# Layer 0 attention: exponentials grouped by tile of context, one addition for both tiles, another order on VectorE

## The chip, the cores and the metric

The kernel runs on one core of a Trainium2 chip. The metric is the time of one execution in device microseconds (us). A core has a matrix engine (TensorE, in the profile PE, its weight loads PEld), a vector engine (VectorE, DVE), a scalar engine for activations (ScalarE, ACT), a general engine (GpSimd, POOL) and a queue engine that here issues most transfers (SyncE, SP). Matmuls write into PSUM, 128 partitions with 8 banks of 512 fp32 each; VectorE and ScalarE read it, GpSimd doesn't. The other working memory is SBUF.

## What is computed

Two transformer layers on 16 batch elements of 256 tokens and 256 channels, all in fp32. Each layer has a self-attention, a cross-attention to a context of 256 tokens, and a feed-forward part, all with residuals. Layer 0, which the change is about, has 16 heads of 64 channels with rotary embedding:

```
def _attn(xq, ctx, wq, wkv, wo, bo):
    q = _heads(xq @ wq)
    k, v = jnp.split(ctx @ wkv, 2, axis=-1)
    k = _heads(k)
    v = _heads(v)
    q = _rope(q, sq, cq)
    k = _rope(k, sk, ck)
    sim = jnp.einsum('bhnd,bhmd->bhnm', q, k) * DH ** (-0.5)
    a = jax.nn.softmax(sim, axis=-1)
    o = jnp.einsum('bhnm,bhmd->bhnd', a, v)
    ...
    return o @ wo + bo

attn_in = _adaln(x, cond, ...)
x = _attn(attn_in, attn_in, sa_wq, sa_wkv, sa_wo, sa_bo) + x
cross_in = _adaln(x, cond, ...)
x = _attn(cross_in, _ln(context, ...), ca_wq, ca_wkv, ca_wo, ca_bo) + x
h = jax.nn.gelu(ffn_in @ ff_w1 + ff_b1, approximate=False)
x = h @ ff_w2 + ff_b2 + x
```

## The kernel before

The program is a sequence of six phases: self-attention, cross-attention and feed-forward of layer 0, then the same of layer 1. A phase has 16 jobs, one for each batch element. The main loop walks over steps; an attention job has two steps (s = 0, 1), a feed-forward job four. So layer 0 attention is 64 steps: 0 to 31 of self-attention, 32 to 63 of cross-attention. The order of the instructions on each engine is the order in which the program emits them, written out by hand; the semaphores between engines follow from the tiles (and PSUM banks) that instructions read and write. PSUM is one tile, `banks`, and the program names the bank of every product.

Scores are transposed: keys lie on partitions, in NT = 2 tiles of context of 128 keys, and the 256 queries along the free dimension. A unit u is four heads; a job has four units, a step handles two, u = 2s and 2s + 1.

- **`stage_s` (L585), the scores of a unit.** 64 matmuls (L598; here and below as the profile counts them, which shows each fp32 matmul twice) of 32 rows by 64 columns, for four heads into four banks: head h goes to bank `at + h`, the context's tile t into the columns t * 256 to t * 256 + 255. The loops run over t, then the half of the channels, then key group and head. The first unit of a step has banks 0 to 3, the second 4 to 7. Then two exponentials (L610), one for each pair p of heads: each reads two whole banks (1024 elements a partition) and writes a half tile `pr` of [P, 2, NT, N]. There are four such buffers. In layer 1 the first pair of every other unit is done head by head, which makes three exponentials.
- **`stage_t` (L614)** adds the two tiles of context for a pair of heads (L619, 512 elements) into half of `both` [P, 4, N]. **`stage_turn` (L621, L625)** transposes `both` in blocks of 32 into `squares`, and **`stage_reduce` (L629, L632)** sums each block's rows into `rows`, the softmax denominators. `both` and `squares` have one buffer each. All are on VectorE.
- **`layer0_sums` (L659)** multiplies `pr` by the values, 32 matmuls (L667) for a unit, into banks 4 and 5, and ScalarE copies the result out (L674). **`sum_up` (L634)** folds the denominators of the job before on PE, inverts them on VectorE (L641), and sends them by SP through memory to be spread (L644, L647). **`scale` (L651, L656)** multiplies by them on GpSimd.
- **`stage_rotary` (L539)** makes queries and keys for the unit of the following step, by products (L82, in `product`) into bank `2 * e + half`: the first unit e = 0 in banks 0 and 1, the second in banks 2 and 3. The keys come first, into columns 256 to 511 (`pq[:, 1, :]`), then the queries. For self-attention that is 64 matmuls for a unit; for cross-attention a part of the keys' product is made ahead by `start_keys` (L527, matmuls L534), 8 matmuls for a unit, right behind the scores. VectorE multiplies by cosine and sine (L555, two for each call, into `m0` and `m1`, two buffers each), and after the second half GpSimd adds and subtracts (L563, two for a unit) into `qk`.
- **`scores(i)` (L1057)** runs `stage_s` for both units of a step, and then `start_keys` for the step behind it where that is cross-attention.
- **`finish_folded` (L946)** in odd steps multiplies the job before by the output weights with seven block products (L82, `folded_w` and `wo` in the profile) in banks 4 and 5, and VectorE adds them to x (L958 to L965). The factors are made by GpSimd (`fold_inner`, L944).
- **`pair_hidden` (L802)**, in the feed-forward phases, has three sums in the buffers of `pr`: `copy` and `six` in one half tile, `seven` in another.

The part of the main loop for layer 0 attention sets the order in a step: VectorE gets two additions, the transpose, two L555, an addition, two L555, an addition, four L555, the reduction, the transpose, the reduction, and then `finish_folded`'s additions (odd steps) or the next job's moments (even steps).

Of the kernel before, what the change touches and what calls it, by code (L numbers as in the profile page):

```python
# [10 lines left out]
F32 = mybir.dt.float32  # L11
I32 = mybir.dt.int32
AF = mybir.ActivationFunctionType
ALU = mybir.AluOpType
AX = mybir.AxisListType

P = 128
N = 256
# [5 lines left out]
NT = N // P  # L24
# [19 lines left out]
def fast(ctx: ExitStack, tc: tile.TileContext, a: dict, out: bass.AP, flag):  # L44
# [4 lines left out]
    nc = tc.nc  # L49
# [6 lines left out]
    work = ctx.enter_context(tc.tile_pool(name="work", bufs=2))  # L56
# [5 lines left out]
    banks = psum.tile([P, 8, 512], F32, name="banks")  # L62
# [521 lines left out]

    def stage_s(job, u, at):  # L585

        key = job["key"]
        pair = job["qk"].pop(u)
        for t in range(NT):
            for half in range(2 if job["layer"] == 0 else 1):  # L590
                for g, h in [(g, h) for g in range(2) for h in range(4)]:
                    r = slice(32 * h, 32 * h + 32)
                    keys = slice(t * P + 64 * g, t * P + 64 * g + 64)
                    if job["layer"] == 0:
                        lhs, rhs = pair[half][r, 1, keys], pair[half][r, 0, :]
                    else:
                        lhs, rhs = pair[1][r, keys], pair[0][r, :]
                    nc.tensor.matmul(  # L598
                        banks[64 * g : 64 * g + 64, at + h, t * N : (t + 1) * N], lhs, rhs,
                        start=(half == 0), stop=(half == 1 or job["layer"] == 1),  # L600
                    )
        prs = []
        for p in range(2):
            pr = work.tile([P, 2, NT, N], F32, tag="pr", name=f"pr_{key}_{u}_{p}", bufs=4)
            sc = banks[:, at + 2 * p : at + 2 * p + 2, :].rearrange("p h (t n) -> p h t n", n=N)

            parts = 2 if job["layer"] == 1 and u % 2 == 0 and p == 0 else 1
            for i in range(parts):
                one = slice(i, i + 1) if parts == 2 else slice(0, 2)
                nc.scalar.activation(pr[:, one], sc[:, one], AF.Exp, scale=0.125 if job["layer"] == 0 else 0.25)  # L610
            prs.append(pr)
        job["pr"][u] = prs

    def stage_t(job, u, p):  # L614

        pr = job["pr"][u][p]
        if p == 0:
            job["both"] = work.tile([P, 4, N], F32, tag="both", name=f"both_{job['key']}_{u}", bufs=1)
        nc.vector.tensor_tensor(job["both"][:, 2 * p : 2 * p + 2, :], pr[:, :, 0, :], pr[:, :, 1, :], ALU.add)  # L619

    def stage_turn(job, u):  # L621

# [6 lines left out]
    def stage_reduce(job, u):  # L629
        if u == 0:  # L630
            job["rows"] = work.tile([P, 4, 32], F32, tag="inv", name=f"rows_{job['key']}")
        nc.vector.tensor_reduce(job["rows"][:, u, :], job.pop("squares"), AX.X, ALU.add)  # L632
# [25 lines left out]

    def layer0_sums(job, u, at):  # L659

        key, v, prs = job["key"], job["v"], job["pr"].pop(u)
        o = bank(at, 2, N)
        for half in range(2):
            for t in range(NT):
                for h in range(4):
                    col = (4 * u + h) * 64 + 32 * half
                    nc.tensor.matmul(  # L667
                        o[32 * h : 32 * h + 32, half, :], v[:, t, col : col + 32], prs[h // 2][:, h % 2, t, :],
                        start=(t == 0), stop=(t == NT - 1),
                    )  # L670
        if u % 2 == 0:
            job["halves"].append(work.tile([P, 4, N], F32, tag="part", name=f"raw_{key}_{u}", bufs=4))
        raw = job["halves"][-1][:, 2 * (u % 2) : 2 * (u % 2) + 2, :]
        nc.scalar.copy(raw, o)  # L674
        job["raw"].append(raw)

    def layer1_sums(job, c, e, at):

        key, v, prs = job["key"], job["v"], job["pr"].pop(2 * c + e)
        o = bank(at, N)  # L680
        for t in range(NT):
            for h in range(4):
                nc.tensor.matmul(  # L683
                    o[32 * h : 32 * h + 32], v[:, t, 4 * c + h, 32 * e : 32 * e + 32],
                    prs[h // 2][:, h % 2, t, :], start=(t == 0), stop=(t == NT - 1),
                )

        if c == 0 and e == 0:  # L690
            job["parts"].append(work.tile([P, 4, N], F32, tag="part", name=f"oT_{key}", bufs=4)[:, 0:2, :])
            job["sums"] = work.tile([P, N], F32, tag="inv", name=f"sums_{key}")
        raw, sums = job["parts"][0][:, c, :], job["sums"]
        if e == 0:
            nc.scalar.activation(raw, o, AF.Copy, scale=mask[:, 0:1])
        else:
            nc.vector.scalar_tensor_tensor(raw, o, mask[:, 1:2], raw, ALU.mult, ALU.add)
        eighth = mask[:, 4 - 2 * e + c : 5 - 2 * e + c]
        if c == 0 and e == 0:
            nc.scalar.activation(sums, o, AF.Copy, scale=eighth)  # L700
        else:
            nc.vector.scalar_tensor_tensor(sums, o, eighth, sums, ALU.mult, ALU.add)
# [99 lines left out]
    def pair_hidden(job, pair, part):  # L802


        key, half = job["key"], job["b"] % 2
        mine = slice(2 * half, 2 * half + 2)
        if part == 0:
            job["places"] = x, y, z = [bank(next_bank(), 2, N) for _ in range(3)]
            job["sums"] = [work.tile([P, 2, 2, N], F32, tag="pr", name=f"sums{i}_{key}", bufs=4) for i in range(2)]
            copy, six = (job["sums"][0][:, i] for i in range(2))  # L810
            block_products(job, x, 1, True)
            block_products(job, y, 6, True)
            block_products(job, z, 5, True)
            nc.scalar.copy(copy, x)
            nc.vector.tensor_tensor(six, y, copy, ALU.add)
            if half == 0:
                for one in pair:
                    if one["b"] % 4 < 2:
                        g = work.tile([P, 2, 4, N], F32, tag="v", name=f"g_{one['key']}")
                        one["halves"] = [g[:, 0], g[:, 1]]  # L820
                    else:
                        one["halves"] = [
                            work.tile([P, 4, N], F32, tag="part", name=f"g{i}_{one['key']}", bufs=4) for i in range(2)
                        ]
            return
        x, y, z = job["places"]
        copy, six = (job["sums"][0][:, i] for i in range(2))
        seven = job["sums"][1][:, 0]
        (top, bottom), (top2, bottom2) = ([h[:, mine, :] for h in one["halves"]] for one in pair)
        if part == 1:  # L830
            block_products(job, x, 2, False)
            block_products(job, y, 7, False)
            for c in range(2):
                gelu(job, top[:, c, :], x[:, c, :], 2 * half + c)
            nc.vector.tensor_tensor(seven, y, copy, ALU.add)
            nc.vector.tensor_tensor(bottom2, z, seven, ALU.add)
        else:
            block_products(job, y, 4, False)
            block_products(job, z, 3, False)
            for c in range(2):  # L840
                gelu(job, bottom2[:, c, :], bottom2[:, c, :], 4 + 2 * half + c)
            nc.vector.tensor_tensor(bottom, y, copy, ALU.add)
            nc.vector.tensor_tensor(top2, z, six, ALU.add)
            for c in range(2):
                gelu(job, bottom[:, c, :], bottom[:, c, :], 4 + 2 * half + c)
            for c in range(2):
                gelu(job, top2[:, c, :], top2[:, c, :], 2 * half + c)
# [264 lines left out]
    for i, (j, s) in enumerate(steps):  # L1112
        job = jobs[j]
        ffn, layer0 = job["kind"] == "ffn", job["layer"] == 0
# [25 lines left out]
        if ffn and layer0 and job["b"] in (2, 5, 8):  # L1140
            at = phases[3 + job["b"] // 3]
# [8 lines left out]
        if ffn:  # L1150
# [32 lines left out]
            if s == 1:  # L1183
                if layer0 and b in (3, 6, 9):
                    at = phases[2 + b // 3]
# [48 lines left out]
        elif layer0:  # L1234
            then = attention(i + 1, 0)
            if leaving and s == 1 and nxt["kind"] == "ffn":
                fold_input_weights(nxt["phase"], nc.gpsimd)
            stage_t(job, 2 * s, 0)
            stage_t(job, 2 * s, 1)
            stage_turn(job, 2 * s)  # L1240
            rotary(then, 0, 0)
            stage_t(job, 2 * s + 1, 0)
            rotary(then, 0, 1)
            if late is not None and s == 1 and then:
                fold_inner(late, nc.gpsimd, 7, 6)
# [1 line left out]
                sum_up(late, 6)  # L1247
            if make_mod:
                make_mod["mod"] = make_mod["make_mod"](6)
            stage_t(job, 2 * s + 1, 1)  # L1250
            rotary(then, 1, 0)
            rotary(then, 1, 1)
            if leaving and s == 0:
                load_phase(job["p"] + 1, "last")
            for e in range(2):
                layer0_sums(job, 2 * s + e, 4 + e if then else e)
            stage_reduce(job, 2 * s)
            stage_turn(job, 2 * s + 1)
            stage_reduce(job, 2 * s + 1)
            if late is not None and s == 1:  # L1260
# [670 lines left out]
```

## Time and profile before

| | |
|---|---|
| three executions | 2175.39, 2180.14, 2180.74 us (median 2180.14) |
| the profiled execution | 2174.7 us, span from first to last instruction 2172.9 us |
| mean granted TensorE clock | 0.999 |
| L610, the 1024-element exponentials of layer 0 and layer 1 | 448, 1035 ns each |
| L610, the 512-element exponentials of layer 1 | 128, 595 ns each |
| L619, the additions of 512 elements | 256, 867 ns each; minimum 620, median 680 |
| L625 transpose, L632 reduction, 1024 elements | 128 each, 1246 and 1214 ns |
| L555, 512 elements out of PSUM | 512, 679 ns each |
| L563 on GpSimd | 256, 1379 ns each |

A row of the profile's groups gives the line, the engine, the operation, the tiles written and read, the shape, the count, the busy time and the mean of one; a timeline row gives start and length in us from the span's start, and in brackets the idle time of the engine ahead of it and what ended that. "issue" stands for idle time in which the profile shows nothing that was waited for. An activation's length includes some overlap with the one ahead of it: two in a row take 1.94 us. Ends of matmuls are modelled.

### The profile page before, as it was taken

The numbers are of one execution on the slowest core, as the hardware profiler recorded it, in microseconds if no ns is written. First come the engines' busy times: TensorE is split into PE (matmuls) and PEld (weight loads), VectorE is DVE, ScalarE is ACT, GpSimd is POOL, SyncE is SP. The second block draws the span as 40 slices with busy tenths as digits, with TensorE's granted clock in tenths as the row PEclk, the third lists the DMA queues.
The fourth block names the chain that finished last, engine by engine and source line by source line (L and its number), as shares of the span: only waits on it lengthen the run. The fifth ranks groups of instructions, "written<-read, shape, count | busy, mean of one in ns | idle before, by whom it ended". The sixth has DMA issues, their size and how long they took to land.

```text
span 2172.9 us, 110193 instructions
## 1 busy us (share of the span) xinstructions
PE 2154.7 (99%) x50112; PEld 1437.1 (66%) x50112; DVE 1688.5 (78%) x3108; ACT 870.1 (40%) x1362; POOL 1240.9 (57%) x1174
## 2 busy tenths in 40 slices
PE   9999999999999999999999999999999999999998
PEld 5666666666665666666666667998556665656787
DVE  6876777777888889888889887774777777777875
ACT  3323233233233233332333334443666666664432
POOL 3766656656657867677676767662232323235673
PEclk9999999999999999999999999999999999999999
DMA  6110010011123221121211123221211232223221
GB/s 194 49 38 22 23 42 22 23 29 36 27 74 86 66 58 44 42 60 35 61 41 44 43 62 99 56 44 25 64 43 39 48 102 63 59 48 78 74 64 39
DMA packets 307030, 117.69 MB, mean 54 GB/s; under 512 B 243364, under 2 KB 289784, under 8 KB 306424
## 3 DMA queue, kind: packets, MB, share of 16 engines
q1 hardware_dynamic: 306008, 110.02, 20.5%
q8 instruction: 394, 6.46, 1.3%
q14 instruction: 84, 0.69, 0.1%
q10 hardware_dynamic: 544, 0.52, 0.1%
HBM read 77.14 MB, written 33.29 MB: 51 GB/s over the span
## 4 chain that ended last, share of the span: by engine, by line
PE 92%; POOL 2%; DVE 2%; DMA 2%; issue 1%; SPq 1%; ACT 0%; DVEq 0%; POOLq 0%; ACTq 0%
PE banks L82 59%; PE banks L598 16%; PE banks L667 9%; PE banks L683 5%; PE banks L534 1%; PE banks L501 1%; POOL raw L656 1%; DMA spread<-sums_seen 0%; DVE m L555 0%; DMA fetched<-turned 0%; DMA sums_seen<-inv 0%; SPq L388 0%; POOL qk L563 0%; POOL folded L944 0%; POOL folded L869 0%
## 5 line engine op out<-in xcount | busy, mean ns | idle before, releaser
L610 ACT ACTIVATE pr<-banks 128x1024 f32<-128x1024 f32 x576 | 487.4, 937 | 415.3 <-PE banks L598 211.9
L563 POOL TENSOR_TENSOR qk<-m,m 128x512 f32<-128x512 f32 x256 | 347.8, 1379 | 302.6 <-DVE m L555 210.7
L555 DVE TENSOR_TENSOR m<-banks,rope 128x512 f32<-128x512 f32 x512 | 324.2, 679 | 85.7 <-POOL qk L563 81.4
L619 DVE TENSOR_TENSOR both<-pr 128x512 f32<-128x512 f32 x256 | 218.9, 867 | 107.9 <-ACT pr L610 107.5
L674 ACT COPY raw<-banks 128x512 f32<-128x512 f32 x128 | 75.2, 587 | 467.3 <-PE banks L667 443.1
L598 PE MATMUL banks<-qk 32*64 32x256 f32 x8192 | 240.7, 377 | 3.0 <-DVE x L961 1.8
L667 PE MATMUL banks<-pr,v 128*32 128x256 f32 x4096 | 233.2, 379 | 0.0
L598 PEld LDWEIGHTS banks<-qk 32*64 32x64 f32 x8192 | 184.1, 131 | 63.7 <-issue 22.4
L667 PEld LDWEIGHTS banks<-pr,v 128*32 128x32 f32 x4096 | 132.9, 110 | 88.7 <-ACT pr L610 0.7
L656 POOL TENSOR_TENSOR raw<-raw,spread 128x512 f32<-128x512 f32 x128 | 162.7, 1304 | 19.7 <-DMA spread<-sums_seen 19.3
L725 POOL TENSOR_TENSOR oT<-oT,spread 128x256 f32<-128x256 f32 x64 | 45.8, 737 | 206.0 <-DVE spread L724 206.0
L625 DVE STREAM_TRANSPOSE squares<-both 128x1024 f32<-128x1024 f32 x128 | 159.4, 1246 | 4.4
L632 DVE TENSOR_REDUCE rows<-squares 128x32 f32<-128x1024 f32 x128 | 155.4, 1214 | 2.2
L451 POOL TENSOR_TENSOR x<-x,bo_b 128x256 f32<-128x256 f32 x96 | 73.0, 781 | 121.2 <-DVE xh L363 121.2
L82 PE MATMUL banks<-hT,wk_sa 128*32 128x256 f32 x2048 | 134.7, 381 | 0.0
L683 PE MATMUL banks<-pr,wide_v 128*32 128x256 f32 x2048 | 134.3, 379 | 0.0
L82 PE MATMUL banks<-hT,wq_ca 128*32 128x256 f32 x2048 | 133.9, 379 | 0.0
L82 PE MATMUL banks<-hT,wq_sa 128*32 128x256 f32 x2048 | 133.9, 379 | 0.0
L355 POOL TENSOR_TENSOR rstd<-ve,neg_half 128x2 f32<-128x2 f32 x95 | 73.0, 769 | 101.0 <-DVE ve L353 97.6
L944 POOL TENSOR_TENSOR folded<-raw,raw 128x512 f32<-128x512 f32 x90 | 127.8, 1448 | 2.4
L900 DVE TENSOR_TENSOR x<-banks,x 128x256 f32<-128x256 f32 (+2 forms) x150 | 79.7, 531 | 63.2 <-PE banks L82 57.0
L598 PE MATMUL banks<-q,k 32*64 32x256 f32 x4096 | 127.8, 381 | 0.0
(225 smaller groups left out, 4020.8 us busy)
## 6 DMA issues: line engine op xcount, KB each, us to landing
turned<-blocks SPq DMA_DIRECT2D x380, 64.0 KB
fetched<-turned SPq DMA_DIRECT2D x380, 64.0 KB
spread<-sums_seen SPq DMA_DIRECT2D x128, 128.0 KB
x<-in_x SPq DMA_DIRECT2D x16, 256.0 KB
fetched_c<-turned_c SPq DMA_DIRECT2D x64, 64.0 KB
cT<-in_ctx_turned SPq DMA_DIRECT2D x16, 256.0 KB
out<-x SPq DMA_DIRECT2D x15, 256.0 KB
ctx<-in_ctx SPq DMA_DIRECT2D x16, 192.0 KB
```

The lines of the kernel that those rows point to most:

```text
L82: nc.tensor.matmul(out[cut], lhsT[:, cut], rhs, start=start, stop=stop, **more)
L555: nc.vector.tensor_tensor(m, pq, rope[:, s : s + 1, :].to_broadcast([P, 2, N]), ALU.mult)
L563: nc.gpsimd.tensor_tensor(r, x, y, (ALU.subtract, ALU.add)[out])
L598: nc.tensor.matmul(banks[64 * g : 64 * g + 64, at + h, t * N : (t + 1) * N], lhs, rhs, start=(half == 0), stop=(half == 1 or job["layer"] ...
L610: nc.scalar.activation(pr[:, one], sc[:, one], AF.Exp, scale=0.125 if job["layer"] == 0 else 0.25)
L619: nc.vector.tensor_tensor(job["both"][:, 2 * p : 2 * p + 2, :], pr[:, :, 0, :], pr[:, :, 1, :], ALU.add)
L625: nc.vector.transpose(job["squares"].rearrange("p b k -> p (b k)"), job.pop("both").rearrange("p h n -> p (h n)"))
L632: nc.vector.tensor_reduce(job["rows"][:, u, :], job.pop("squares"), AX.X, ALU.add)
L656: nc.gpsimd.tensor_tensor(part, part, spread[:, u : u + 1, :].to_broadcast([P, 2, N]), ALU.mult)
L667: nc.tensor.matmul(o[32 * h : 32 * h + 32, half, :], v[:, t, col : col + 32], prs[h // 2][:, h % 2, t, :], start=(t == 0), stop=(t == NT - 1),
L683: nc.tensor.matmul(o[32 * h : 32 * h + 32], v[:, t, 4 * c + h, 32 * e : 32 * e + 32], prs[h // 2][:, h % 2, t, :], start=(t == 0), stop=(t ...
L944: eng.tensor_tensor(folded[m], *sums[m])
```

## The change

- The four half tiles `pr` become two whole ones, [P, 4, NT, N]. In layer 0 the two exponentials of a unit go by tile of context t: each reads, for all four heads, the 256 columns of tile t, and writes `pr[:, :, t, :]`. In layer 1 the pieces are the same three or two as before.
- `stage_t` adds both tiles of all four heads in one operation of 1024 elements.
- In a step, the second unit's addition stands behind the second L555 pair as one operation, and the first unit's reduction moves up to right behind it, ahead of the last four L555.
- The readers of `pr` index the whole tile. The feed-forward sums lie in strided halves of one tile: `copy` in heads 0 and 1 of t = 0, `six` in heads 2 and 3 of t = 0, `seven` in heads 0 and 1 of t = 1.

```diff
@@ -584,39 +584,35 @@
 
     def stage_s(job, u, at):
 
-        key = job["key"]
+        key, layer0 = job["key"], job["layer"] == 0
         pair = job["qk"].pop(u)
         for t in range(NT):
-            for half in range(2 if job["layer"] == 0 else 1):
+            for half in range(2 if layer0 else 1):
                 for g, h in [(g, h) for g in range(2) for h in range(4)]:
                     r = slice(32 * h, 32 * h + 32)
                     keys = slice(t * P + 64 * g, t * P + 64 * g + 64)
-                    if job["layer"] == 0:
+                    if layer0:
                         lhs, rhs = pair[half][r, 1, keys], pair[half][r, 0, :]
                     else:
                         lhs, rhs = pair[1][r, keys], pair[0][r, :]
                     nc.tensor.matmul(
                         banks[64 * g : 64 * g + 64, at + h, t * N : (t + 1) * N], lhs, rhs,
-                        start=(half == 0), stop=(half == 1 or job["layer"] == 1),
+                        start=(half == 0), stop=(half == 1 or not layer0),
                     )
-        prs = []
-        for p in range(2):
-            pr = work.tile([P, 2, NT, N], F32, tag="pr", name=f"pr_{key}_{u}_{p}", bufs=4)
-            sc = banks[:, at + 2 * p : at + 2 * p + 2, :].rearrange("p h (t n) -> p h t n", n=N)
-
-            parts = 2 if job["layer"] == 1 and u % 2 == 0 and p == 0 else 1
-            for i in range(parts):
-                one = slice(i, i + 1) if parts == 2 else slice(0, 2)
-                nc.scalar.activation(pr[:, one], sc[:, one], AF.Exp, scale=0.125 if job["layer"] == 0 else 0.25)
-            prs.append(pr)
-        job["pr"][u] = prs
-
-    def stage_t(job, u, p):
-
-        pr = job["pr"][u][p]
-        if p == 0:
-            job["both"] = work.tile([P, 4, N], F32, tag="both", name=f"both_{job['key']}_{u}", bufs=1)
-        nc.vector.tensor_tensor(job["both"][:, 2 * p : 2 * p + 2, :], pr[:, :, 0, :], pr[:, :, 1, :], ALU.add)
+        pr = job["pr"][u] = work.tile([P, 4, NT, N], F32, tag="pr", name=f"pr_{key}_{u}")
+        sc = banks[:, at : at + 4, :].rearrange("p h (t n) -> p h t n", n=N)
+        if layer0:
+            for t in range(NT):
+                nc.scalar.activation(pr[:, :, t, :], sc[:, :, t, :], AF.Exp, scale=0.125)
+        else:
+            for one in [slice(0, 1), slice(1, 2), slice(2, 4)] if u % 2 == 0 else [slice(0, 2), slice(2, 4)]:
+                nc.scalar.activation(pr[:, one], sc[:, one], AF.Exp, scale=0.25)
+
+    def stage_t(job, u):
+
+        pr = job["pr"][u]
+        job["both"] = work.tile([P, 4, N], F32, tag="both", name=f"both_{job['key']}_{u}", bufs=1)
+        nc.vector.tensor_tensor(job["both"], pr[:, :, 0, :], pr[:, :, 1, :], ALU.add)
 
     def stage_turn(job, u):
 
@@ -658,14 +654,14 @@
 
     def layer0_sums(job, u, at):
 
-        key, v, prs = job["key"], job["v"], job["pr"].pop(u)
+        key, v, pr = job["key"], job["v"], job["pr"].pop(u)
         o = bank(at, 2, N)
         for half in range(2):
             for t in range(NT):
                 for h in range(4):
                     col = (4 * u + h) * 64 + 32 * half
                     nc.tensor.matmul(
-                        o[32 * h : 32 * h + 32, half, :], v[:, t, col : col + 32], prs[h // 2][:, h % 2, t, :],
+                        o[32 * h : 32 * h + 32, half, :], v[:, t, col : col + 32], pr[:, h, t, :],
                         start=(t == 0), stop=(t == NT - 1),
                     )
         if u % 2 == 0:
@@ -676,13 +672,13 @@
 
     def layer1_sums(job, c, e, at):
 
-        key, v, prs = job["key"], job["v"], job["pr"].pop(2 * c + e)
+        key, v, pr = job["key"], job["v"], job["pr"].pop(2 * c + e)
         o = bank(at, N)
         for t in range(NT):
             for h in range(4):
                 nc.tensor.matmul(
                     o[32 * h : 32 * h + 32], v[:, t, 4 * c + h, 32 * e : 32 * e + 32],
-                    prs[h // 2][:, h % 2, t, :], start=(t == 0), stop=(t == NT - 1),
+                    pr[:, h, t, :], start=(t == 0), stop=(t == NT - 1),
                 )
 
 
@@ -806,8 +802,8 @@
         mine = slice(2 * half, 2 * half + 2)
         if part == 0:
             job["places"] = x, y, z = [bank(next_bank(), 2, N) for _ in range(3)]
-            job["sums"] = [work.tile([P, 2, 2, N], F32, tag="pr", name=f"sums{i}_{key}", bufs=4) for i in range(2)]
-            copy, six = (job["sums"][0][:, i] for i in range(2))
+            job["sums"] = work.tile([P, 4, 2, N], F32, tag="pr", name=f"sums_{key}")
+            copy, six = (job["sums"][:, 2 * i : 2 * i + 2, 0, :] for i in range(2))
             block_products(job, x, 1, True)
             block_products(job, y, 6, True)
             block_products(job, z, 5, True)
@@ -824,8 +820,8 @@
                         ]
             return
         x, y, z = job["places"]
-        copy, six = (job["sums"][0][:, i] for i in range(2))
-        seven = job["sums"][1][:, 0]
+        copy, six = (job["sums"][:, 2 * i : 2 * i + 2, 0, :] for i in range(2))
+        seven = job["sums"][:, 0:2, 1, :]
         (top, bottom), (top2, bottom2) = ([h[:, mine, :] for h in one["halves"]] for one in pair)
         if part == 1:
             block_products(job, x, 2, False)
@@ -1235,11 +1231,9 @@
             then = attention(i + 1, 0)
             if leaving and s == 1 and nxt["kind"] == "ffn":
                 fold_input_weights(nxt["phase"], nc.gpsimd)
-            stage_t(job, 2 * s, 0)
-            stage_t(job, 2 * s, 1)
+            stage_t(job, 2 * s)
             stage_turn(job, 2 * s)
             rotary(then, 0, 0)
-            stage_t(job, 2 * s + 1, 0)
             rotary(then, 0, 1)
             if late is not None and s == 1 and then:
                 fold_inner(late, nc.gpsimd, 7, 6)
@@ -1247,14 +1241,14 @@
                 sum_up(late, 6)
             if make_mod:
                 make_mod["mod"] = make_mod["make_mod"](6)
-            stage_t(job, 2 * s + 1, 1)
+            stage_t(job, 2 * s + 1)
+            stage_reduce(job, 2 * s)
             rotary(then, 1, 0)
             rotary(then, 1, 1)
             if leaving and s == 0:
                 load_phase(job["p"] + 1, "last")
             for e in range(2):
                 layer0_sums(job, 2 * s + e, 4 + e if then else e)
-            stage_reduce(job, 2 * s)
             stage_turn(job, 2 * s + 1)
             stage_reduce(job, 2 * s + 1)
             if late is not None and s == 1:
```

## The prediction

> **What bounds the kernel now.** I read the page's busy shares and chain, then the chain in order of time over one ordinary step, then PE's waits, then the timeline around the place that the change edits.
>
> ```profile
> PE 2154.7 (99%) x50112; PEld 1437.1 (66%) x50112; DVE 1688.5 (78%) x3108; ACT 870.1 (40%) x1362; POOL 1240.9 (57%) x1174
> PE 92%; POOL 2%; DVE 2%; DMA 2%; issue 1%; SPq 1%; ACT 0%; DVEq 0%; POOLq 0%; ACTq 0%
> 413.00 3.64 PE banks L598 x128
> 416.64 7.04 PE banks L82 x128
> 423.68 3.45 PE banks L667 x64
> 427.14 6.11 PE banks L82 x224
> 433.25 3.64 PE banks L598 x128
> ```
>
> The last five lines are one self-attention step of 20.25 us: scores, rotary products, value sums, output products, next scores, all on PE and end to end. ScalarE, VectorE and GpSimd enter the end only where they make PE wait. So a saved VectorE or ScalarE microsecond is worth nothing by itself, and a new PE wait costs its full length, once per step. Layer 0 attention has 64 such steps.
>
> The timeline at the head of a self step (first three lines) and of a cross step (last three):
>
> ```profile
> 412.93 3.71 PE L598 MATMUL banks<-qk 32*64 32x256 f32 x128
> 415.05 3.77 ACT L610 ACTIVATE pr<-banks 128x1024 f32<-128x1024 f32 x4 [1.39 <-PE banks L598]
> 416.57 1.07 PE L82 MATMUL banks<-hT,wk_sa 128*32 128x256 f32 x16
> ...
> 801.13 3.77 ACT L610 ACTIVATE pr<-banks 128x1024 f32<-128x1024 f32 x4 [6.50 <-issue]
> 802.66 0.21 PEld L534 LDWEIGHTS banks<-cT,wk_ca 64*64 64x64 f32 x8 [0.38 <-issue]
> 803.12 0.21 PEld L534 LDWEIGHTS banks<-cT,wk_ca 64*64 64x64 f32 x8 [0.25 <-ACT pr L610]
> ```
>
> Count from the start of the scores. Before, the first exponential (banks 0 and 1) starts at 2.12 us and the second (banks 2 and 3) follows. PE's next product goes into banks 0 and 1 at 3.64, and needs the first exponential alone, which is long over. In the cross step the second group of L534 goes into banks 2 and 3, and there PE does wait for the second exponential: the list of waits has it 29 times, 7.4 us in all.
>
> **Part 1: exponentials by tile.** Each of the two new exponentials reads half of all four banks. Two questions decide.
>
> When can the first start? By its columns, after the first 32 of the unit's 64 matmuls. The trace says that readers here wait for the whole bank:
>
> ```profile
> 430.45 2.80 PE L82 MATMUL banks<-folded_w,folded 128*32 128x128 f32 x96
> 430.77 0.42 DVE L958 TENSOR_TENSOR x<-x,banks 128x256 f32<-128x256 f32 x1 [0.52 <-PE banks L82]
> ...
> 838.30 0.42 DVE L959 TENSOR_TENSOR x<-banks,x 128x256 f32<-128x256 f32 x1
> 838.75 0.69 DVE L961 TENSOR_TENSOR x<-banks,x 128x512 f32<-128x512 f32 x1
> 839.59 0.61 PE L598 MATMUL banks<-qk 32*64 32x256 f32 x2 [0.16 <-DVE x L961]
> ```
>
> L958 reads columns 0 to 255 of its bank, finished when PE went on to the next weights at 428.70; yet VectorE idled 0.52 us until 430.77, just after the products in columns 256 to 511 ended. The other way round, the score matmul at 839.59 writes columns 0 to 255 of bank 4, whose last reader by columns, L959, ended at 838.72; it started when L961, the reader of columns 256 to 511, ended at 839.44. So the first new exponential still waits for all 64 matmuls and starts at 2.12.
>
> The Trainium skill, PSUM — Partial Sum Buffer, section "PSUM bank collisions raise a hardware error", speaks against an early start too: it asks that PSUM be guarded by bank and quadrant, not by address, since two engines in one bank collide even on disjoint columns. By that page the sum is the one below; by columns alone it would be that of the second rival.
>
> When is bank 0 free? Only after the second exponential, since the rotary product's first write (`pq[:, 1, :]`) falls on columns that it reads. Two of them take 1.94 us in a row (a timeline entry at 839.55 shows "1.94 ... x2"), so in the self step the second ends at 415.05 + 1.94 = 416.99. From the end of an exponential to the released weight load is 0.05 (801.13 + 1.94 = 803.07, load at 803.12), and a matmul released so starts about 0.03 behind its load, against 0.00 otherwise. PE goes on at 417.07 in place of 416.57: **0.50 us lost in each of the 31 self steps (0 to 30), 15.5 us.** PE already has 0.38 of idle weight load there ("issue"), but that lies before 416.57, so it hides nothing of this.
>
> In a cross step the wait moves from the second group of L534 to the first. The 16 matmuls without a wait take 1.02 (842.42 to 843.44 in a step where the exponentials were early), so L82 follows at 803.12 + 1.02 = 804.14 in place of 803.71: 0.43, in the 29 steps that have this wait now: **12.5 us.**
>
> The price of the new form is not in the trace. The nearest row is the present one, also 1024 elements, 1.03 us median. From above: two 512-element exponentials of layer 1 at 0.595 make 1.19, 0.15 more each, 0.30 for the pair, 60 x 0.30 = 18 us. From below: nothing, since the fastest 1024-element ones take 1.02. I take the nearest row. The ScalarE: Activation LUTs page of the Trainium skill (section "What ACT_TABLE_LOAD costs") prices an activation by its element count alone, which would give the same value; no run here shows it for four strided runs.
>
> **Part 2: one addition in place of two.** Two L619 of 512 elements (minimum 0.62, median 0.68) become one of 1024. The 1024-element transpose and reduction take 1.25 and 1.21, so it costs 1.21 to 1.36 in place of 1.24 to 1.36: a saving of 0 to 0.1, 128 times, beside PE. It must wait for both exponentials, so it starts 0.95 us later (417.0, not 416.10) and ends about 0.3 later. What is late next is the transpose, then the first multiplication L555 (419.24 becomes about 419.55); no PE product needs that bank before the next scores, 13 us on.
>
> **Part 3: VectorE's order.** The reduction of the first unit (1.21 us) goes ahead of the last four L555, where VectorE now idles:
>
> ```profile
> 831.85 2.55 DVE L555 TENSOR_TENSOR m<-banks,rope 128x512 f32<-128x512 f32 x4 [1.17 <-POOL qk L563]
> 834.31 1.21 DVE L632 TENSOR_REDUCE rows<-squares 128x32 f32<-128x1024 f32 x1
> ```
>
> It fills that gap, the four L555 stay within some 0.3 to 0.9 us, and the tail behind them (transpose, reduction, L958 to L965) comes about 1.25 earlier. Queued behind the four L555 is GpSimd's second pair of L563 and, in even steps, the scaling (5.0 us) and L944 (3.8). In a cross step that pair ends at 815.83 and is wanted by the scores of the second unit at about 819.7, so even 0.9 later is covered; the four-microsecond slack is the cover, and beyond it PE would wait. `sum_up`'s reciprocal comes ahead of the addition, so SP's writes (L644, L647) and the loads L388 behind them are not later. The DMAs are the same.
>
> The earlier tail pays where PE waits for it: three cross steps, at 679.4, 758.4 and 837.5, where the score stretch takes 5.80, 5.44 and 4.97 in place of 3.64 (L961 and L965 late by 2.16, 1.80, 1.33). With a tail 1.25 earlier, and PE 0.43 later itself, 0.48, 0.12 and 0 are left; below 0.43 the new wait for the exponential stands in. Gain 1.68 + 1.37 + 0.90 = 4.0. The output products before 679.41 also wait 0.56 for GpSimd, which PE's own delay covers: **4.5 us gained.** In ordinary odd steps the tail is not waited for, and the gain is nothing.
>
> **Part 4: the rest.** Layer 1's exponentials keep their pieces, and the feed-forward sums take strided halves of one tile. Strided VectorE work costs the same (L961, four runs, 0.692; the contiguous L842 0.691): nothing. Two whole `pr` buffers in place of four halves: the next exponential into a buffer comes 7 us after its last reader, L667: nothing.
>
> **Sum:** 15.5 + 12.5 - 4.5 = 23.5 us. The profiled execution took 2174.7 (span 2172.9), so 2198.2; it lies 5.4 below the median of the runs shown, which gives 2203.6. I predict **2203**.
>
> **Rivals.**
> - *PE waits as above, and the new form is dear* (18 us more, +41.5): 2221. For it: the unseen pattern over four banks. Against it: the present form also crosses a bank boundary, and strided rows on VectorE cost nothing extra. 8%.
> - *The first exponential starts early, by columns* (this ends on the other side). It would start at about 2.12 - 0.91 = 1.21, the second at 2.13 when its matmuls end, over at 3.15 and before PE's 3.64. No PE wait, the 4.5 us of part 3 remain: 2175.6, or -0.2%. It decides once the second exponential ends before 3.59. Against it: L958 and L961 above. For it: only that other columns are read. 12%; about half of it within 0.3% and half faster, if more of VectorE's lateness goes.
> - *The new wait is swallowed*, so that the change does nothing: PE would need slack between 416.57 and the next scores, and the chain shows none. About 2180. 5%.
> - *My main case*, 75%, its own range 2194 to 2214: release lags between 0.05 and the 0.15 from L961's end to the matmul it released (60 x 0.1 = 6 us up), a gain of 0 to 8 in part 3, and 5 between the profiled execution and the slowest run.
>
> About 0.3% (6.5 us) is what a measurement of this kernel can tell from no change. Faster comes from half of the second rival and a little of the third, 0.08; within 0.3% from the rest of both, 0.09; slower 0.83. The range of 8 in 10 is the main case's own, widened up halfway to the dear form and down by some us: 2189 to 2218.
>
> **What would show it.** In the profile after: a wait of PE's weight loads for the exponential at the first rotary product of a self step, about 30 of some 0.1 us idle or more, with PE going on about 0.5 us later after the scores; L534's wait on its first group; self steps of 20.75 in place of 20.25 us; ScalarE's first exponential still about 2.1 us behind the scores; VectorE's gap before the last four L555 gone; the three long score stretches near 4.1 us or less. It is wrong if the first exponential starts near 1.2 us, if self steps stay at 20.25, or if the new exponential takes 1.2 us.

## The result, and the profile after

The changed kernel takes 2202.77 us (median of 5, 2202.37 to 2203.02), the kernel before 2179.37 (median of 5): the ratio is 1.0112, 95% interval 1.0101 to 1.0123, so it is slower by 23.4 us. The profiled execution took 2202.93, with a span of 2201.1 against 2172.9.

The page after, busy shares and chain by engine:

```profile
PE 2158.4 (98%) x50112; PEld 1416.4 (64%) x50112; DVE 1649.8 (75%) x2980; ACT 870.1 (40%) x1362; POOL 1265.9 (58%) x1174
PE 91%; ACT 4%; issue 1%; DVE 1%; DMA 1%; POOL 1%; SPq 0%; ACTq 0%; DVEq 0%; POOLq 0%
```

VectorE has 128 instructions and 39 us of work less, GpSimd 25 us more (the mean of its L563 goes from 1379 to 1494 ns), ScalarE exactly the same 870.1 us, PE the same matmuls. What is new is that ScalarE stands in the chain with 4%, where it had 0%. The chain in order of time shows where, in one self step:

```profile
421.94 2.00 PE banks L598 x64
423.94 0.03 ACTq L606
423.96 0.04 issue
424.01 1.95 ACT pr L606 x2
425.95 0.04 issue
426.00 7.11 PE banks L82 x128
433.11 3.45 PE banks L663 x64
436.56 6.11 PE banks L82 x224
442.68 1.43 PE banks L598 x41
```

Before, this chain ran from 128 score matmuls straight into L82. Now it leaves PE after the first unit's 64, follows both exponentials (L606, L610 before), and comes back to PE at 426.00. The second unit's scores lie beside the exponentials and no longer count.

The timeline at the head of that step, and at the head of a cross step:

```profile
421.87 3.71 PE L598 MATMUL banks<-qk 32*64 32x256 f32 x128
424.01 3.77 ACT L606 ACTIVATE pr<-banks 128x1024 f32<-128x1024 f32 x4 [1.42 <-PE banks L598]
425.98 1.29 DVE L615 TENSOR_TENSOR both<-pr 128x1024 f32<-128x1024 f32 x1 [7.44 <-ACT pr L606]
426.00 1.07 PE L82 MATMUL banks<-hT,wk_sa 128*32 128x256 f32 x16 [0.42 <-ACT pr L606]
...
813.43 3.71 PE L598 MATMUL banks<-qk 32*64 32x256 f32 x128
815.57 3.77 ACT L606 ACTIVATE pr<-banks 128x1024 f32<-128x1024 f32 x4 [6.54 <-issue]
817.56 1.09 PE L534 MATMUL banks<-cT,wk_ca 64*64 64x256 f32 x16 [0.42 <-ACT pr L606]
```

The first exponential starts 2.14 us behind the scores (2.12 before): it does not start early. PE goes on 4.13 us behind them in both kinds of step; before, it was 3.64. The list of waits has the two places with their counts:

```profile
PEld banks L534 <- ACT pr L606: 27.3, 32, 0.9
PEld banks L82 <- ACT pr L606: 27.0, 31, 0.9
```

L82 waits behind the scores of steps 0 to 30, L534 behind those of step 31, the last self step, and of steps 32 to 62: 63 of the 64 steps wait. On average each wait is 0.87 and 0.85 us of idle time of the weight loads; the 0.38 that lay there before as "issue" is in it, and in the self step the difference, 0.49, is what PE lost.

The groups of the two new forms:

```profile
L606 ACT ACTIVATE pr<-banks 128x1024 f32<-128x1024 f32 x256 | 241.8, 1029 | 243.2 <-issue 169.7 <-DVE blocks L373 27.1 <-PE banks L598 24.8
L615 DVE TENSOR_TENSOR both<-pr 128x1024 f32<-128x1024 f32 x128 | 171.4, 1339 | 194.0 <-ACT pr L606 193.9
```

An exponential over four strided runs costs 1.03 us, the same as over two whole banks.

### The profile page after: what moved, and what is told of

It reads as the page before. It is cut to its first block, busy times and chain, and to the rows that moved or that the text cites. A ratio compares the mean times of both kernels' runs of the same rounds, so it can differ in the third digit from the quotient of the medians.

```text
span 2201.1 us, 109791 instructions
## 1 busy us (share of the span) xinstructions
PE 2158.4 (98%) x50112; PEld 1416.4 (64%) x50112; DVE 1649.8 (75%) x2980; ACT 870.1 (40%) x1362; POOL 1265.9 (58%) x1174
## 4 chain that ended last, share of the span: by engine, by line
PE 91%; ACT 4%; issue 1%; DVE 1%; DMA 1%; POOL 1%; SPq 0%; ACTq 0%; DVEq 0%; POOLq 0%
PE banks L82 60%; PE banks L598 13%; PE banks L663 10%; PE banks L679 5%; ACT pr L606 3%; PE banks L534 2%; PE banks L501 1%; DMA fetched<-turned 0%; ACT v L507 0%; SPq L388 0%; POOL folded L865 0%; POOL qk L563 0%; DMA rows<-in_rows 0%; DMA spread<-sums_seen 0%; POOL x L451 0%
## 5 line engine op out<-in xcount | busy, mean ns | idle before, releaser
L563 POOL TENSOR_TENSOR qk<-m,m 128x512 f32<-128x512 f32 x256 | 377.4, 1494 | 303.2 <-DVE m L555 290.0
L555 DVE TENSOR_TENSOR m<-banks,rope 128x512 f32<-128x512 f32 x512 | 324.0, 681 | 21.1 <-POOL qk L563 9.1
L606 ACT ACTIVATE pr<-banks 128x1024 f32<-128x1024 f32 x256 | 241.8, 1029 | 243.2 <-issue 169.7
L615 DVE TENSOR_TENSOR both<-pr 128x1024 f32<-128x1024 f32 x128 | 171.4, 1339 | 194.0 <-ACT pr L606 193.9
L609 ACT ACTIVATE pr<-banks 128x1024 f32<-128x1024 f32 (+1 forms) x320 | 245.5, 864 | 167.7 <-PE banks L598 167.7
L82 PE MATMUL banks<-hT,wk_sa 128*32 128x256 f32 x2048 | 134.8, 381 | 12.9 <-ACT pr L606 12.9
L82 PE MATMUL banks<-hT,wq_sa 128*32 128x256 f32 x2048 | 134.0, 379 | 0.0
L82 PE MATMUL banks<-hT,wq_ca 128*32 128x256 f32 x2048 | 133.9, 379 | 0.0
```

The costliest lines, as they stand in the source:

```text
L82: nc.tensor.matmul(out[cut], lhsT[:, cut], rhs, start=start, stop=stop, **more)
L555: nc.vector.tensor_tensor(m, pq, rope[:, s : s + 1, :].to_broadcast([P, 2, N]), ALU.mult)
L563: nc.gpsimd.tensor_tensor(r, x, y, (ALU.subtract, ALU.add)[out])
L606: nc.scalar.activation(pr[:, :, t, :], sc[:, :, t, :], AF.Exp, scale=0.125)
L615: nc.vector.tensor_tensor(job["both"], pr[:, :, 0, :], pr[:, :, 1, :], ALU.add)
```

## The experiments

All kernels are variants of the changed one. Where a ratio is given it is against the kernel before, run on the same chip (median 2176.19 us beside the first four kernels, 2176.91 beside the last three). Lengths of single steps come from one profiled execution of each kernel.

The theory: PE's end-to-end chain is broken once per step, at the first product behind the scores, because each new exponential holds part of all four banks, so that banks 0 and 1 come free one exponential later. The rivals: VectorE's part of the change makes the loss (the one addition waits for both exponentials); the new form costs in itself; and, on the question of the first start, a bank is handed over by columns.

**Pairs again.** Only the exponentials go back to two whole banks each:

```diff
-            for t in range(NT):
-                nc.scalar.activation(pr[:, :, t, :], sc[:, :, t, :], AF.Exp, scale=0.125)
+            for two in (slice(0, 2), slice(2, 4)):
+                nc.scalar.activation(pr[:, two], sc[:, two], AF.Exp, scale=0.125)
```

> The changed kernel with the exponentials of layer 0 by pair of heads again (two whole banks each); the whole pr tile, the one addition and VectorE's new order stay. Theory (the loss is PE waiting at the first product behind the scores, because both exponentials hold banks 0 and 1): the wait is gone, the gain of the earlier VectorE tail stays, 2179.4 - 4.5 + 1.3 (the activation table's load that the changed kernel exposes once in layer 1) = about 2176; self steps of 20.25 us, ordinary cross odd steps of 19.6. Rival (the loss comes from the one addition, which starts later, or from VectorE's new order): stays near 2203, self steps near 20.74.

Measured: 2172.49 us, ratio 0.9984 (0.9975 to 0.9994). Self steps take 20.25 us again and cross odd steps 19.59. The whole loss, and a little more, comes from these two lines. The rest of the change is a small gain.

**Exponentials by tile only.** VectorE's part goes back:

```diff
-            stage_t(job, 2 * s)
+            stage_t(job, 2 * s, 0)
+            stage_t(job, 2 * s, 1)
...
+            stage_t(job, 2 * s + 1, 0)
...
-            stage_t(job, 2 * s + 1)
-            stage_reduce(job, 2 * s)
+            stage_t(job, 2 * s + 1, 1)
...
+            stage_reduce(job, 2 * s)
             stage_turn(job, 2 * s + 1)
```

> The changed kernel with VectorE's work as before: an addition for each pair of heads, in the old places, the reduction of the first unit behind the value sums. Only the exponentials by tile (and the whole pr tile) are left of the change. Theory: the new waits stay whole and the 4.5 us of the earlier tail are lost: 2203 + 4 to 5 = about 2207, self steps of 20.74. Rival (VectorE's part makes the loss): back at about 2180.

Measured: 2203.84 us, ratio 1.0150 (1.0099 to 1.0201), 27.7 above the kernel before beside it, where the whole change is 23.4. The self steps take 20.74 and wait 31 times, as in the changed kernel, with VectorE's old order and old additions. The interval is wide (one of the four executions took 2223.56, the others 2201.84 to 2203.96), and the medians say little on VectorE's part. The steps say more: from the first scores of step 0 to those of step 63 this kernel takes 1275.04 us, only 1.36 more than the changed one (1273.68), not 4 to 5. Where PE itself comes some 0.45 later in every step, VectorE's tail is less late for it; steps 32, 36 and 40 take 20.33, 19.91 and 19.88 against 19.70, 19.30 and 19.30. So most of the loss is the exponentials', and VectorE's part is worth little beside it.

**By tile in the second unit alone.** Half of the new exponentials, those on banks 4 to 7:

```diff
-        if layer0:
+        if layer0 and u % 2 == 0:
+            for two in (slice(0, 2), slice(2, 4)):
+                nc.scalar.activation(pr[:, two], sc[:, two], AF.Exp, scale=0.125)
+        elif layer0:
             for t in range(NT):
                 nc.scalar.activation(pr[:, :, t, :], sc[:, :, t, :], AF.Exp, scale=0.125)
```

> The changed kernel with the exponentials by pair of heads for the first unit of a step (banks 0 to 3) and by tile for the second (banks 4 to 7). Theory: banks 4 to 7 are next written by the value sums, 7 us after the scores, so holding them costs nothing: about 2176, the same as with pairs throughout. Rival (each exponential by tile costs in itself, by its pattern or its wait): half of the exponentials, half of the loss, about 2190.

Measured: 2173.14 us, ratio 0.9982 (0.9973 to 0.9992), the same as with pairs throughout. Its timeline shows both forms in one step:

```profile
413.09 3.71 PE L598 MATMUL banks<-qk 32*64 32x256 f32 x128
415.20 1.94 ACT L606 ACTIVATE pr<-banks 128x1024 f32<-128x1024 f32 x2 [1.39 <-PE banks L598]
416.73 1.07 PE L82 MATMUL banks<-hT,wk_sa 128*32 128x256 f32 x16
417.03 1.95 ACT L609 ACTIVATE pr<-banks 128x1024 f32<-128x1024 f32 x2
```

L606 are the pairs, L609 the tiles: 1.94 and 1.95 us for two. PE goes on 3.64 us behind the scores, as it did before. So neither the form nor its count costs anything; what costs is that the banks which the next product needs are held.

**An early start.** Each tile's exponential is issued ahead of the other tile's matmuls:

```diff
         for t in range(NT):
             for half in range(2 if layer0 else 1):
...
+            if layer0:
+                nc.scalar.activation(pr[:, :, t, :], sc[:, :, t, :], AF.Exp, scale=0.125)
```

> The changed kernel with each tile's exponential issued right behind that tile's score matmuls, ahead of the other tile's. Theory (a bank is handed over whole, not by columns): the second tile's matmuls wait for the first tile's exponential, about 1.35 us in each unit, and the first unit's second exponential is over by the time PE comes to the rotary products: about 2.5 us longer in each of 63 steps, some 2360 in all. Rival (by columns): the first exponential runs beside the second tile's matmuls, PE waits nowhere, about 2176.

Measured: 2358.02 us, one execution. One unit in its timeline:

```profile
469.07 1.12 PE L600 MATMUL banks<-qk 32*64 32x256 f32 x32
470.35 1.02 ACT L605 ACTIVATE pr<-banks 128x1024 f32<-128x1024 f32 x1 [0.55 <-PE banks L600]
471.42 1.99 PE L600 MATMUL banks<-qk 32*64 32x256 f32 x64 [1.23 <-ACT pr L605]
472.65 1.95 ACT L605 ACTIVATE pr<-banks 128x1024 f32<-128x1024 f32 x2 [1.28 <-PE banks L600]
```

The exponential does start 1.28 us behind the scores, and the second tile's matmuls, into other columns of the same banks, stand until it ends at 471.37. So in both orders of issue a bank is handed over whole. These waits are set by the program's own semaphores; no run here has an exponential beside matmuls in its own banks, so what the chip would do without the waits is not shown.

**VectorE's part, split.** Two kernels take "pairs again" apart: one keeps the new order with two additions of 512 elements in place of one of 1024, the other keeps the one addition with the reduction in its old place.

```diff
# order only
-        nc.vector.tensor_tensor(job["both"], pr[:, :, 0, :], pr[:, :, 1, :], ALU.add)
+        for two in (slice(0, 2), slice(2, 4)):
+            nc.vector.tensor_tensor(job["both"][:, two], pr[:, two, 0, :], pr[:, two, 1, :], ALU.add)
# one addition only
             stage_t(job, 2 * s + 1)
-            stage_reduce(job, 2 * s)
...
+            stage_reduce(job, 2 * s)
             stage_turn(job, 2 * s + 1)
```

> pairs_again with two additions of 512 elements for each unit in place of one of 1024, in the new places; the reduction of the first unit stays ahead of the last four multiplications. Theory (the earlier VectorE tail is made by the order): the steps 32, 36 and 40 stay within 0.2 us of pairs_again (19.72, 18.84, 18.83), the time within 0.5. Rival (the one addition makes the gain): those steps go back towards 20.97, 20.62 and 20.14, 4 us more.

> pairs_again with the reduction of the first unit back in its old place behind the value sums; the one addition of 1024 elements stays behind the second pair of multiplications. Theory: the tail is earlier only by the addition that no longer stands between the two pairs, about 0.65 us and not 1.25: steps 32, 36 and 40 about 0.65 shorter than before the change (20.3, 20.0, 19.5), so some 2 us more than pairs_again. Rival (the one addition makes the whole gain): as pairs_again.

Measured: order only 2175.58, ratio 0.9992 (0.9983 to 1.0002); one addition only 2175.72, ratio 0.9997 (0.9987 to 1.0007). Both expectations fell. The length in us of the three cross steps where PE waited for VectorE's tail, by the starts of their scores:

| step | before | pairs again | order only | one addition only | the change |
|---|---|---|---|---|---|
| 32 | 20.97 | 19.72 | 19.73 | 20.97 | 19.70 |
| 36 | 20.62 | 18.84 | 19.36 | 19.53 | 19.30 |
| 40 | 20.14 | 18.83 | 20.68 | 20.16 | 19.30 |

Neither half alone has the whole gain: their medians lie 4.0 and 4.1 us above that of "the table's load ahead" below, which ran beside them (2171.60) and saves 1.25 us elsewhere. In step 32 the order alone has it, in step 36 each half has a part, in step 40 neither has any. The column of order only needs care: its profiled execution was the slowest of its ten, 2179.48 against the median of 2175.58. The step before step 40, around the addition in question, in "pairs again", then order only, then one addition only:

```profile
825.39 1.20 DVE L615 TENSOR_TENSOR both<-pr 128x1024 f32<-128x1024 f32 x1
825.61 3.38 POOL L563 TENSOR_TENSOR qk<-m,m 128x512 f32<-128x512 f32 x2 [2.57 <-DVE m L555]
826.52 1.21 DVE L628 TENSOR_REDUCE rows<-squares 128x32 f32<-128x1024 f32 x1
```

```profile
828.79 2.37 DVE L616 TENSOR_TENSOR both<-pr 128x512 f32<-128x512 f32 x2
829.01 3.29 POOL L563 TENSOR_TENSOR qk<-m,m 128x512 f32<-128x512 f32 x2 [3.17 <-DVE m L555]
831.08 1.21 DVE L629 TENSOR_REDUCE rows<-squares 128x32 f32<-128x1024 f32 x1
```

```profile
827.49 1.21 DVE L615 TENSOR_TENSOR both<-pr 128x1024 f32<-128x1024 f32 x1
829.87 2.54 DVE L555 TENSOR_TENSOR m<-banks,rope 128x512 f32<-128x512 f32 x4 [1.17 <-POOL qk L563]
```

An addition of VectorE with both inputs in SBUF and GpSimd's L563 hold each other off. With one addition (first fence), VectorE is ahead: 1.20 us, and GpSimd's two operations take 3.38 in place of some 2.55. With two additions (second fence), GpSimd's first operation gets in between, and the pair takes 2.37. The reduction, which has one input, runs beside GpSimd at 1.21 throughout. With one addition but the reduction behind (third fence), VectorE still idles the 1.17 us in which it waits for GpSimd's result. So the move of the reduction fills the gap, and the one addition keeps GpSimd from opening another of the same size. The sums over the whole run agree: VectorE's L555 idles behind L563 for 81.4 us before, 87.2 in one addition only, 14.6 in "pairs again" and 6.7 in order only, and an addition of 512 elements takes 1176 ns on average in order only, 867 before.

The Trainium skill, SBUF — State Buffer, section "Who interferes with whom", describes just this: a VectorE instruction with two inputs in SBUF contends with a GpSimd instruction that reads SBUF, over a pair of ports that the two engines share under an exclusive lock. The rows above agree: the second of the two additions took 1.78 us and ended 0.55 us after GpSimd's operation did, by the trace at 831.16 and 830.61.

**The table's load ahead.** Every kernel above with the whole `pr` tile, the changed one too, loses 1.25 us at one place: PE's first product behind layer 1's first scores. ScalarE there, before and after the change:

```profile
1494.37 1.28 ACT L610 ACT_TABLE_LOAD   x1
1497.54 2.00 ACT L610 ACTIVATE pr<-banks 128x512 f32<-128x512 f32 x3 [1.89 <-PE banks L598]
```

```profile
1522.11 1.28 ACT L609 ACT_TABLE_LOAD   x1 [3.21 <-PE banks L598]
1523.40 2.92 ACT L609 ACTIVATE pr<-banks 128x512 f32<-128x512 f32 x4
```

Before, the load of the table for the exponential ran while ScalarE waited for the scores; after, it stands behind that wait. Why the whole tile moves the wait ahead of the load was not tried. The variant is "pairs again" with one tiny exponential more, at the end of layer 0's last feed-forward step:

```diff
+                if then:
+                    soon = stat.tile([P, 1], F32, tag="ve", name="exp_soon")
+                    nc.scalar.activation(soon, neg_half[:, 0:1], AF.Exp)
```

> pairs_again with one more tiny exponential on ScalarE, at the end of layer 0's last feed-forward step, ahead of layer 1's first scores (its result is not used). Theory: the activation table's load (1.28 us) stood behind the first exponential's wait for the scores, and the tiny one pulls it ahead of them: PE's wait at layer 1's first rotary product falls from 1.64 to about 0.4 us, and the time by 1.25 us against pairs_again. Rival (that wait comes from the whole pr tile or its buffers): no change.

Measured: 2171.60 us, ratio 0.9975 (0.9965 to 0.9984), the lowest median of all kernels here and below both the kernel before and the changed one. ScalarE now loads early:

```profile
1490.91 1.28 ACT L1228 ACT_TABLE_LOAD   x1
1492.20 0.20 ACT L1228 ACTIVATE exp_soon<-neg_half 128x1 f32<-128x1 f32 x1
1494.15 3.83 ACT L609 ACTIVATE pr<-banks 128x512 f32<-128x512 f32 x5 [1.74 <-PE banks L598]
```

Counted from layer 1's first scores, PE comes to that matmul 1.25 us earlier than in "pairs again" (1.91 against 3.16), and the longest wait of L82 for L609 falls from 1.6 to 0.4. The medians differ by 0.9 with overlapping intervals, so the gain is shown at its place and not in the total.

## Why the prediction was right

- **The bound.** PE's chain had no slack: nearly every self step after is longer by 0.49 us (20.25 to 20.74, 21.07 to 21.56), and nothing of it is made good within the step.
- **The first start (part 1).** Read from L958 and L961, and right: 2.14 us behind the scores after, and "an early start" shows the same handing over of whole banks, as this program's semaphores do it, from the other side.
- **The wait (part 1).** 0.50 per self step was forecast, 0.49 measured, in 31 steps, 15.2 us. In cross steps 0.43 was forecast, 0.45 (odd) and 0.47 (even) measured. That the held banks make it, and nothing else, is shown by "pairs again", "exponentials by tile only" and "by tile in the second unit alone" together.
- **The new form's price (part 1).** The nearest row, 1.03 us, held to 1.03; the dear form is out.
- **The one addition and the order (parts 2 and 3).** The term of 4.5 us was of the right size for VectorE's part without the new waits: "pairs again" is 4.0 us shorter than before from the first scores of step 0 to those of step 63 (1244.68 against 1248.70). With them it was too large: steps 32, 36 and 40 are 1.27, 1.32 and 0.84 shorter than before, 3.4 in all against the 4.0 forecast, and PE still goes on 4.53 us behind the scores of step 32, not 4.1. Nor is all of that VectorE's doing: in "exponentials by tile only", with VectorE's old order, the same steps are already 1.6 shorter in all than before, where PE itself comes later. VectorE's part is the other 1.8 there, and 1.36 over all steps. The attribution was in part wrong too. The prediction gave the whole 1.25 us of the tail to the reduction's new place and 0 to 0.1 to the one addition. That holds for step 32, but the two splits show that each alone leaves step 40 where it was or worse. What failed is the step that priced an addition without what GpSimd does beside it: 867 ns mean against a median of 680 in the trace of before was the sign. Of the 0.56 for the output products before step 32 a little over half was got: step 31 took 20.28, where 20.14 less 0.56 plus 0.43 gives 20.01. With VectorE's old order it took 20.04, so PE's delay does cover the 0.56 there; why 0.24 is left with the new order was not tried.
- **The rest (part 4).** Priced at nothing, and it cost 1.25 us: the table's load, above.
- **The sum.** From the first scores of step 0 to those of step 63 the profiled executions differ by 24.98 us (1248.70 to 1273.68), against 23.5 forecast. By steps that is 15.4 more in the self steps 0 to 30 (15.5 forecast), 0.1 more in step 31, 12.9 more in the 28 ordinary cross steps and 3.4 less in the three long ones. The spans differ by 28.2: 1.25 more at the table's load and some 3.5 more in layer 1's feed-forward part, less about 1.5 in small pieces elsewhere. Of the 3.5, about 1.4 is one wait of PE's weight loads for VectorE's first folded inputs, 4.5 us in place of 3.1. Most of the rest is the clock: the 32 matmuls behind that wait take 3.64 us at a granted clock of 0.50, where before they took 1.93 at 1.00. The wait is 4.5 in "exponentials by tile only" and "order only" too, and 3.1 to 3.4 in "pairs again", "by tile in the second unit alone", "one addition only" and "the table's load ahead", with the same code there; the low clock comes with the wait of 3.1 in "pairs again" and not with that of 3.2 in "the table's load ahead". The causes of both were not tried and stay open. The profiled execution of before was also 4.7 below its median, that of after 0.2 above its own, so the medians differ by 23.4. Errors of opposite sign lie under the hit of 2203: the mechanism and the size per step were right, the closeness of the total was luck.

## What to carry to other kernels

On a chain in which one engine runs end to end, and where buffers are handed over by whole PSUM banks as here, a split of an evacuation (the operations that read finished products out of PSUM) is judged by which banks each piece lets go, and when the bound engine needs the first of them: cut along the banks that are wanted next, not across them. When every piece touches every bank, all of them come free only with the last piece, however cheap it is. Where VectorE and GpSimd work from SBUF side by side, the price of an operation can depend on which of the two is ahead, so a move and a merge are worth trying together as well as apart.

## What the runs showed of the hardware that was not expected

- A VectorE addition of 512 elements with both inputs in SBUF took 0.67 us ahead of GpSimd's L563 and 1.78 behind its start; GpSimd's L563 took 2.13 in place of 1.29 where VectorE was ahead. The reduction next to it kept its 1.21.
- The activation table's load of 1.28 us can land behind the wait of the activation that needs it, and then counts in full: 1.25 us of PE time here.
- The granted clock can fall for a few us behind a wait of PE in one run and not in another: 32 matmuls took 3.64 us at 0.50 in the changed kernel, 1.93 at 1.00 before, behind waits of 4.5 and 3.1 us. After nearly equal waits it was 0.51 in "pairs again" (3.1 us) and 1.00 in "the table's load ahead" (3.2 us), so the wait's length alone does not decide it here.
